# The tiles' transposes moved from TensorE to VectorE and a way through DRAM, in an attention and feed-forward kernel

## The chip, the cores and the metric

The kernel runs on one core of a Trainium2 chip. The metric is device time of one execution in microseconds (us). TensorE does the matrix products, VectorE and ScalarE work on tiles in on-chip memory (SBUF, 128 partitions) and on the matmuls' accumulators (PSUM, banks of 128 x 512 float32), GpSimd does elementwise work, and SyncE (SP) issues the transfers to and from DRAM, which 16 DMA engines carry out. Each engine works through its own instructions in order and waits on semaphores for the others.

## The reference

Everything is float32, with a batch of B = 2, T = 1024 tokens and C = 1024 channels:

```python
x = x + attn_a(layernorm(x))    # 32 heads of 32, causal, rope; plus a gated softmax over a prefix of 10 tokens
x = x + ffn(layernorm(x))
x = x + attn_b(layernorm(x))    # 8 heads of 16, not causal, softmax divided by sqrt(128)
x = x + ffn(layernorm(x))       # the same weights again

def attn_a(x):
    q, k, v = split(x @ w_attn.T, 3)                # 1024 columns each, in 32 heads
    y = softmax(causal(rope(q) @ rope(k).T / sqrt(32))) @ v
    y = y + gating * softmax(rope(q) @ ak.T / sqrt(1024)) @ av   # ak, av from the prefix
    return y @ w_proj.T

def ffn(x):
    base = x @ W_base.T + b_base
    w = sparsemax(x @ W_router.T + b_router)        # 8 experts
    h = einsum('bsd,edr->bser', x, lora_A)          # rank 16
    return base + einsum('bser,bse,ero->bso', h, w, lora_B)

def attn_b(x):
    q, k = (x @ Wqk_w.T + Wqk_b)                    # 128 columns each: 8 heads of 16
    v = x @ Wv_w.T + Wv_b                           # 128 columns
    return (softmax(q @ k.T) / sqrt(128) @ v) @ Wo_w.T + Wo_b
```

Every one of the four steps starts with a layer normalization over the channels, whose result has tokens on the partitions. The matrix products that follow contract over channels, so they need it the other way round, with channels on the partitions. How that turn is made is what the change is about.

## The kernel before

**Stages.** A tile is 128 tokens by 1024 channels, so each batch has NT = 8 tiles, and a tile has NC = 8 channel parts of 128. Stage A (attn_a, both batches, 8 groups of heads each) runs to about 1250 us, then its output projection to about 1460, the first feed-forward of batch 0 to about 1590, stage B's projection of batch 0 (`project_b`) to about 1645; from about 1690 attention B runs, with batch 1's first feed-forward and projection and much of the second feed-forward among it, and the end of the second feed-forward fills the time from about 2240.

**The order on TensorE** is written out ahead by a planner. Work around attention (projections, feed-forward) comes as generators which yield the estimated time of each matmul (a column costs COL = 1.7 ns); between attention's own steps `fill.run` takes so much of it. A few jobs are "chores", which are put off until they are due or until `flush` asks for them; a layer normalization's last part is such a chore, and `settle` flushes it. `pin` ties a VectorE instruction behind the latest softmax maximum.

**Two forms of a matmul.** `mm` (L195) issues one matmul of 128 columns of weights (L198) or, where the last thing before was a step of attention, four of 32 columns side by side (L200). `flip` (L202), a transpose by a matmul with the identity, sets it back to the first form. A float32 matmul shows as two records in the profile, so the second form shows as eight.

**Turning a tile.** `transposed` (L281) makes eight transposes by TensorE, in two banks of four (L204), and `evac` (L229) copies each bank into the turned tile, in turn by VectorE (L232) and ScalarE (L234). The turned tile has for every channel part 128 tokens side by side. All 64 tiles of the program are turned so: 16 in stage A, 32 in the two feed-forwards, 16 in stage B. In stage A, batch 1 is normalized early (`normalize_ahead`, L736), stored to DRAM (`xnd`, L741), loaded again (L751) and turned by `second` (L746) between matmuls, paced by `turn_over`.

**Feed-forward** (`ffn`, L1243). It works on pairs of tiles. `fetch` loads, `normalize` normalizes, `turn` (L1264) turns. `hidden` (L1312) makes hp, the experts' hidden values: for each tile eight matmuls with the turned tile's part as weights and 136 columns moving. The base product is made in seven products instead of eight (`seven_added`, L1069, in the order 1, 6, 2, 7, 5, 4, 3): `left_factors` (L1114) forms sums and differences of turned parts on VectorE, and the turned tiles are the weights of products with 512 columns moving. The next pair's tiles are turned inside products 5, 4 and 3.

**Stage B's projection** (`project_b`, L1470). For each tile eight matmuls make bv, with the turned tile's part as weights (L1504), and sixteen make bq, with it as the moving operand (L1525), 128 columns each.

**Transfers.** All are issued from SP, in program order. SP's rows in a profile are issues; a load that waits for something holds those behind it.

Of the kernel before, what the change touches and what calls it, by code (L numbers as in the profile page):

```python
# [20 lines left out]
P = 128  # L21
# [126 lines left out]
def tile_model(ctx: ExitStack, tc: tile.TileContext, d, out: bass.AP):  # L148
# [149 lines left out]


    class Unit:  # L300

# [261 lines left out]

    xnd = [dram.tile([P, C], F32, name=f"xnd{t}") for t in range(NT)]

    def stage_a(wk, big):
# [169 lines left out]
        def normalize_ahead():  # L736

            for t in range(NT + 1):
                if t:
                    settle(f"a1_{t - 1}")  # L740
                    sp.dma_start(xnd[t - 1], xn)  # L741
                if t < NT:
                    xn = layernorm(big, "t4k", x_load(1, t, big, "t4k"), f"a1_{t}", behind=True)
                yield ("norm", t)

        def second():  # L746


            def load(t):
                xn = big.tile([P, C], F32, tag="t4k", name=f"xn1_{t}")  # L750
                sp.dma_start(xn, xnd[t])  # L751
                return xn

            xns = {t: load(t) for t in range(2)}
            for t in range(NT):
                n, i = divmod(t, 4)
                if i == 0:
                    yield None
                    xnT[1, n] = big.tile([P, NC, HF], F32, tag="h16", name=f"xnT1_{n}")
                if t + 2 < NT:  # L760
                    xns[t + 2] = load(t + 2)
                yield from transposed(xns.pop(t), xnT[1, n][:, :, i * P : (i + 1) * P], f"a1_{t}")

        given = [False]
        owed = [0]

        def turn_over():

            owed[0] += 1
            if given[0]:  # L770
                given[0] = False
                return
            while owed[0]:
                owed[0] -= 1
                yield next(turnover)

        def adapter_scores(u):
            given[0] = True
            b, g, n = u.at
# [28 lines left out]
        def late(r, begun):  # L808
            spent = 0.0
            given[0] = False  # L810
            for u, at in begun.items():
                if r - at == 1:
                    spent += adapter_scores(u)
                elif r - at == 4:
                    spent += adapter_rows(u)
            return spent
# [62 lines left out]
        def project_first(b, between):  # L879
            wqk = wqk_at[b, 0]  # L880
            if b == 0:
                yield adapter_parts("k0", lambda c: wqk[:, c, 1, :], P)
            else:
                assert next(turnover) is None
                yield from begin_values(b, 0)
            for n in range(2):
# [6 lines left out]
                for s, key in ((1, "k"), (0, "q")):  # L893
                    qp = next_bank([P, HF], f"{key}p{b}_{n}")
                    for c in range(NC):
                        mm(qp, lhsT=wqk[:, c, s, :], rhs=xh[:, c, :], start=(c == 0), stop=(c == NC - 1))
                        yield HF * COL
                        if b and n == 0 and c % 2:
                            yield from turn_over()
                    rotate(b, 0, key, n, qp)  # L900
                    if b == 0 and n == 0 and key == "k":
                        yield adapter_keys(0)
                if b and n == 0:
                    while owed[0]:
                        owed[0] -= 1
                        yield next(turnover)
                yield ("qk", b, 0, n)
# [4 lines left out]
        def project_blocks(b, g):  # L912
            nm = f"{b}_{g}"
            k, q = st["k", b, g], st["q", b, g]
            if (b, g) == (0, NG - 1):
                assert next(turnover) is None
            halves = {i: (t, n) for i, t, n in ((11, k, 0), (12, k, 1), (21, q, 0), (22, q, 1))}
# [10 lines left out]
            for r in seven(b, nm, st.pop(("f", b, g)), mul, [P, HF], places, lambda x: rotate(b, g, "k", 0, x), settled):  # L928
# [3 lines left out]
                elif r is True:  # L932
                    yield ("qk", b, g, 0)
                else:
                    yield r
                    i += 1
                    if i == 14 and b == 0:
                        yield adapter_keys(g)
                    if (b, g) == (0, NG - 1) and i > 12 and i % 2 == 0:
                        yield from turn_over()  # L940
            while owed[0]:
                owed[0] -= 1
                yield next(turnover)
            yield ("qk", b, g, 1)
# [97 lines left out]
        ahead = normalize_ahead()  # L1042
        turnover = second()
        for b in range(B):
# [198 lines left out]
    def ffn(b, k, src, dst, w, wk, tiles, places, free=lambda: True, there=lambda t: True):  # L1243
# [6 lines left out]
        seq = [t for p in range(0, len(tiles), 2) for t in (tiles[p + 1], tiles[p])]  # L1250
        xs, xns, xts, hws, stores = {}, {}, {}, {}, deque()
        room = kept[2 if k else b]
# [6 lines left out]
        def normalize(i):  # L1259
            t = seq[i]  # L1260
            xns[t] = layernorm(wk, "xn", xs[t], f"f{b}_{k}_{t}", behind=True,
                               then=lambda: pool_add(xs[t], xs[t], w["b_base"]))

        def turn(i, parts=(0, 1), by=None):  # L1264
            t = seq[i]
            settle(f"f{b}_{k}_{t}")
            return transposed(xns[t], place_xt(i) if 0 in parts else xts[t], f"f{b}_{k}_{t}", parts, by)

        def place_xt(i):
            t = seq[i]  # L1270
            xts[t] = room["xt"] if room and i % 3 == 2 else wk.tile([P, NC, P], F32, tag="xt", name=f"xt_f{b}_{k}_{t}", bufs=2)
            return xts[t]

# [68 lines left out]
        def plain(p):  # L1342
            order = [(n, c) for n in range(2) for c in range(NC)]
            order = order[:4] + order[NC:] + order[4:NC]
            for i in range(2):
                t = seq[2 * p + i]
                ops = {}
                for n, c in order:
# [9 lines left out]
                    if (i, n, c) == (0, 1, 1):  # L1358
                        normalize(2)
                    if (i, n, c) == (1, 0, 1):  # L1360
                        while stores:
                            sp.dma_start(*stores.popleft())
                        fetch(3)
                    if (i, n, c) == (1, 1, 5):
                        normalize(3)
                    if i and c == 5:
                        yield from turn(2, (1 - n,))
                    if (i, n, c) == (0, 1, 5):
# [6 lines left out]
                    yield HF * COL  # L1375
            settle(f"f{b}_{k}_{seq[3]}")
            yield from transposed(xns[seq[3]], place_xt(3), f"f{b}_{k}_{seq[3]}", by=(next_bank, next_bank))

        def take_room():
            if not room or (b, k) == (1, 0):  # L1380
                ring, work, more = places()
                room.update(ring=ring, work=work, x=more[:, :2].rearrange("p a c -> p (a c)"),
                            xt=more[:, 2:].rearrange("p a (b c) -> p (a b) c", c=P))
                fill.flush("wb")
# [5 lines left out]
        yield None  # L1390
        normalize(0)
        yield None
        normalize(1)
        yield READY
        if not late_room:
            take_room()
        for i in range(2):
            yield from turn(i, by=(bank, next_bank))
        n_pairs = len(tiles) // 2
        for p in range(n_pairs):  # L1400
# [29 lines left out]
            hwT = []  # L1430
            turns = {(5, 0): (2, 0), (5, 3): (2, 1), (4, 2): (3, 0), (3, 1): (3, 1)}

            def ready(i):
                if i == 6:
                    fill.flush(nm)
                elif i == 5:
                    fill.flush("wb1")
                if not last and i in (6, 7):
                    normalize(2 * p + 2 + (i == 7))

            def also(i, k, dst):
                if not last and (i, k) in turns:
                    j, part = turns[i, k]
                    yield from turn(2 * p + j, (part,))
                if (i, k) == (2, 1):
# [24 lines left out]
    def project_b(b, w, fk, wk, st):  # L1470
        xs, ready = {}, {}

# [4 lines left out]
        def normalize(t):  # L1477
            xn = layernorm(fk, "xn", xs.pop(t), f"b{b}_{t}", behind=True)
            ready[t] = xn, fk.tile([P, NC, P], F32, tag="xt", name=f"xt_b{b}_{t}", bufs=2)

        fetch(0)
        fetch(1)
        yield None
        normalize(0)
        yield READY
        qk = st["qk", b] = wk.tile([P, 2, T], F32, tag=f"qkb{b}", name=f"qk{b}", bufs=1)
        kq = st["kq", b] = wk.tile([P, 2, T], F32, tag=f"kqb{b}", name=f"kq{b}", bufs=1)

        vm = st["vm", b] = wk.tile([P, NT, HB, 2 * EB], F32, tag=f"vm{b}", name=f"vm{b}", bufs=1)
        pool.memset(vm, 0.0)  # L1490
        normalize(1)
        fetch(2)
        fetch(3)
        settle(f"b{b}_0")
        yield from transposed(*ready[0], f"b{b}_0", by=(bank, next_bank))
        for t in range(NT):
            xnT = ready.pop(t)[1]
            if t >= NT - 2:

                yield AHEAD  # L1500
            cols = slice(t * P, (t + 1) * P)
            vp = next_bank([P, P], f"bv{b}_{t}")
# [10 lines left out]
            if t == NT - 2:  # L1513
                yield AHEAD
            if t + 1 < NT:
                settle(f"b{b}_{t + 1}")
                yield from transposed(*ready[t + 1], f"b{b}_{t + 1}", by=(bank, next_bank))
            if t + 2 < NT:
                normalize(t + 2)
            if t + 4 < NT:  # L1520
                fetch(t + 4)
            qp = next_bank([P, 2, P], f"bq{b}_{t}")
# [248 lines left out]
```

## Time and profile before

| | us |
|---|---|
| three runs | 2406.23, 2408.8, 2414.7 |
| median of these | 2408.8 |
| span of the profiled execution | 2407.9 |
| TensorE busy in it | 2351.2 (98%) |
| VectorE, ScalarE, GpSimd busy | 1437.3, 1100.4, 598.6 |
| moved by the DMA engines | 274.70 MB, 114 GB/s on the mean |

A row of a group names the line, the engine, the operation, output <- inputs with their shapes and the count of records; then the busy time of all, the mean of one in ns, and the idle time of the engine just before them with what ended it. Records of matmuls overlap, so the mean of one is longer than the time it takes of the order; a stretch of the timeline shows that.

By stage, the stretches that hold the tiles in question: in the first feed-forward of batch 0 (1460 to 1590 us) TensorE is busy for all of the 130 us, VectorE for 71.91, with the DMA engines at a share of 0.50; in 1855 to 1945 us, attention B with batch 1's projection, 85.00 of 90 and 71.38; in 2270 to 2408, the last feed-forward, 133.44 of 138 and 66.83. Much of SP's time is spent waiting for results to store.

### The profile page before, as it was taken

How to read it: one execution, taken by the hardware profiler on the slowest of the kernel's cores; microseconds unless marked ns; L12 is line 12 of the kernel's file. 1: busy time of each engine (PE TensorE's matmuls, PEld its weight loads, DVE VectorE, ACT ScalarE, POOL GpSimd, SP SyncE). 2: the span in 40 equal slices, each digit the busy share in tenths (PEclk: the TensorE clock that was granted, in tenths of full speed). 3: DMA queues.
4: the chain of work that ended last, by engine and by line, in shares of the span. 5: the costliest groups of instructions: out<-in, count | busy, mean ns of one | idle time of the engine just before them, and what ended most of it. 6: DMA issues, size and time to landing. Idle time of an engine off the chain costs nothing.

```text
span 2407.9 us, 60616 instructions
## 1 busy us (share of the span) xinstructions
PE 2351.2 (98%) x25151; PEld 1077.8 (45%) x25151; DVE 1437.3 (60%) x4317; ACT 1100.4 (46%) x2106; POOL 598.6 (25%) x933
## 2 busy tenths in 40 slices
PE   8999999999999999999999999999999999999999
PEld 4435443455354444445433445575333653233454
DVE  6587666666656666666651246566666765664453
ACT  3346665666565666666652001012455546564100
POOL 1432232222323232223211114202111111122332
PEclk9999999999999999999999999999999999999999
DMA  4443433333243333332312575441332302323543
GB/s 151 141 132 111 136 91 132 98 94 107 90 123 103 92 96 106 88 98 77 133 58 71 174 258 174 159 148 60 121 94 91 112 20 80 105 85 101 175 158 122
DMA packets 174772, 274.70 MB, mean 114 GB/s; under 512 B 16416, under 2 KB 76960, under 8 KB 174496
## 3 DMA queue, kind: packets, MB, share of 16 engines
q1 hardware_dynamic: 174496, 270.83, 35.2%
q8 instruction: 197, 3.23, 0.6%
q14 instruction: 79, 0.65, 0.1%
HBM read 215.19 MB, written 55.57 MB: 112 GB/s over the span
## 4 chain that ended last, share of the span: by engine, by line
PE 89%; DVE 6%; ACT 2%; DMA 1%; issue 1%; POOL 0%; SPq 0%; DVEq 0%; POOLq 0%; ACTq 0%
PE st L411 10%; PE sc L339 8%; PE y_A L433 5%; PE y L200 5%; PE y_f L198 4%; PE z_f L198 4%; PE z L200 4%; PE st L409 3%; PE x_f L198 3%; PE x L200 3%; PE y_v L200 3%; PE y_f L200 3%; PE y_B L433 2%; PE x_f L200 2%; PE y_p L198 2%; DVE pr_A L352 2%
## 5 line engine op out<-in xcount | busy, mean ns | idle before, releaser
L523 ACT ACTIVATE pt<-st 128x1024 f32<-128x1024 f32 (+1 forms) x418 | 425.5, 1018 | 605.8 <-PE st L411 463.6
L360 ACT ACTIVATE pr_A<-pr_A,nmax_A 128x896 f32<-128x896 f32 (+7 forms) x512 | 389.9, 765 | 55.1 <-DVE nmax_A L352 54.5
L352 DVE CUSTOM_DVE_ANT_0 pr_A<-sc,mask 128x512 f32<-128x512 f32 (+3 forms) x512 | 251.2, 537 | 190.2 <-PE st L411 90.7
L339 PE MATMUL sc<-kT,qT 32*128 32x512 f32 (+3 forms) x1536 | 326.1, 521 | 4.8 <-POOL qT L851 3.0
L411 PE MATMUL st<-qT,kT 32*128 32x512 f32 (+3 forms) x1536 | 306.4, 486 | 0.0
L352 DVE CUSTOM_DVE_ANT_0 pr_A<-sc,mask,part_A 128x512 f32<-128x512 f32 (+1 forms) x256 | 156.2, 647 | 145.7 <-PE sc L339 95.0
L418 POOL TENSOR_SCALAR_AFFINE_SELECT pt<-pt 128x256 f32<-128x256 f32 x256 | 105.9, 431 | 469.1 <-ACT pt L523 469.1
L239 POOL TENSOR_TENSOR xf<-xf,b_base 128x256 f32<-128x256 f32 x100 | 74.5, 775 | 417.8 <-DVE xn_f L267 261.9
L360 ACT ACTIVATE pr_B<-pr_B,nmax_B 128x1024 f32<-128x1024 f32 x128 | 145.5, 1141 | 36.4 <-DVE nmax_B L352 36.3
L433 PE MATMUL y_A<-pt,v 128*32 128x512 f32 (+3 forms) x1536 | 157.9, 498 | 0.0
L339 PE MATMUL sc<-kq,qk 32*128 32x512 f32 x512 | 146.5, 649 | 4.6 <-DVE nmax_B L352 3.8
L411 PE MATMUL st<-rows_B,kq 32*128 32x512 f32 x512 | 145.8, 646 | 2.4 <-ACT pt L523 1.7
L411 PEld LDWEIGHTS st<-qT,kT 32*128 32x128 f32 x1536 | 133.6, 185 | 16.3 <-issue 11.3
L409 PE MATMUL st<-rows_A,ones 3*128 3x512 bf16 (+3 forms) x768 | 127.8, 329 | 5.6 <-DVE nmax_A L352 5.0
L352 DVE CUSTOM_DVE_ANT_0 pr_B<-sc,zeros,part_B 128x512 f32<-128x512 f32 x128 | 91.0, 747 | 59.3 <-PE sc L339 59.3
L409 PEld LDWEIGHTS <-ones 3*128 3x128 bf16 x768 | 36.9, 91 | 194.7 <-issue 187.3
L339 PEld LDWEIGHTS sc<-kT,qT 32*128 32x128 f32 x1536 | 113.0, 184 | 18.3 <-POOL qT L851 5.0
L352 DVE CUSTOM_DVE_ANT_0 pr_B<-sc,zeros 128x512 f32<-128x512 f32 x128 | 83.2, 687 | 60.4 <-PE sc L339 60.2
L850 POOL TENSOR_TENSOR qr<-qr,sin 128x256 f32<-128x256 f32 x64 | 61.3, 957 | 220.9 <-DVE qr L846 213.9
L360 ACT ACTIVATION_READ_ACCUMULATOR pr_A<-pr_A,nmax_A 128x1 f32 x512 | 97.2, 190 | 0.0
L200 PE MATMUL y<-tt,wqk 128*32 128x512 f32 x768 | 92.6, 594 | 0.0
L433 PEld LDWEIGHTS y_A<-pt,v 128*32 128x32 f32 x1536 | 33.7, 108 | 118.2 <-issue 109.9
(424 smaller groups left out, 4232.8 us busy)
## 6 DMA issues: line engine op xcount, KB each, us to landing
tt<-td SPq DMA_DIRECT2D x252, 256.0 KB, 2.9
qkb_f<-tf SPq DMA_DIRECT2D x96, 256.0 KB, 3.0
qkb_s<-tf SPq DMA_DIRECT2D x84, 256.0 KB, 2.9
wqk<-in_w_attnT SPq DMA_DIRECT2D x32, 512.0 KB, 5.2
xf<-x SPq DMA_DIRECT2D x25, 512.0 KB, 3.7
xa<-in_x SPq DMA_DIRECT2D x16, 512.0 KB, 6.0
wv<-in_w_attnT SPq DMA_DIRECT2D x8, 1024.0 KB, 5.3
yd<-ys SPq DMA_DIRECT2D x32, 256.0 KB, 2.7
```

Source lines behind the costliest of these rows:

```text
L198: return pe.matmul(out, lhsT=lhsT, rhs=rhs, start=start, stop=stop, skip_group_check=True)
L200: pe.matmul(out[i : i + 32], lhsT=lhsT[:, i : i + 32], rhs=rhs, start=start, stop=stop, skip_group_check=True)
L239: pool.tensor_add(dst[:, i : i + 2 * P], a[:, i : i + 2 * P], b[:, i : i + 2 * P])
L339: yield w * COL, lambda: pe.matmul(dst[:, o : o + w], lhsT=self.qt[rows, qc : qc + P], rhs=self.kt[rows, c0 : c0 + w], start=True, stop=True)
L352: minimum[0] = dve.tensor_tensor_reduce(pr[:, c0 : c0 + w], sc[:, i, o : o + w], m, -self.scale, BIG if c0 == 0 else self.part[:, col], AL ...
L360: tc.keep_in_program_order(act.activation(pr[:, :nk], pr[:, :nk], AF.Exp, bias=self.nmax[:, col], scale=-1.0, accum_out=self.sums[:, col]))
L409: yield w * COL / 4, lambda: pe.matmul(dst[:, o : o + w], lhsT=of["ones"][three, :], rhs=self.rows[three, off : off + w], start=True, stop ...
L411: yield w * COL, lambda: pe.matmul(dst[:, o : o + w], lhsT=self.kt[rows, kb * P : (kb + 1) * P], rhs=rhs, start=self.extra, stop=True)
L418: pool.affine_select(out=dg, in_=dg, compare_op=ALU.is_ge, fill=0.0, base=0, pattern=[[0, 2], [1, P]], channel_multiplier=-1)
L433: pe.matmul(self.y[32 * h : 32 * h + 32, off : off + w], lhsT=self.value(h, kb), rhs=pt[h // 2][:, h % 2, o : o + w], start=self.opens, st ...
L523: act.activation(pt[:, :, low_:wide_], st[:, :, low_:wide_], AF.Exp, scale=ts[0][0].scale)
L850: pool.tensor_mul(qr[:, hs], qr[:, hs], sin[:, cols][:, hs])
```

## The change

56 of the 64 tiles are no longer turned by TensorE: the 8 of batch 1 in stage A, the 32 of the feed-forwards, the 16 of stage B. VectorE transposes the tile in blocks of 32 x 32 (`turned_out`), the result goes to a tile-sized place in DRAM, and it is read back so that the blocks land where a whole transpose needs them.

```diff
+    def turned_out(pl, tag, xn, dst, name, bufs=None, apart=True):
+        d = pl.tile([P, 4, P // 4 * NC], F32, tag=tag, name=f"d_{name}", **({"bufs": bufs} if bufs else {}))
+        blocks = d.rearrange("p b (i c) -> p c b i", c=NC) if apart else d.rearrange("p b (c i) -> p c b i", c=NC)
+        pin(dve.transpose(blocks, xn.rearrange("p (c b i) -> p c b i", b=4, i=32)))
+        sp.dma_start(dst, d.rearrange("p b e -> p (b e)"))
+
+    def turned_in(dst, src):
+        rows = src.rearrange("(a j) (b c i) -> a b j c i", a=4, b=4, i=32)
+        for b in range(4):
+            for a in range(4):
+                sp.dma_start(dst[32 * b : 32 * b + 32, :, 32 * a : 32 * a + 32], rows[a, b])
+
+    def turned_apart(pl, src, name):
+        xt = pl.tile([P, 4, P // 4 * NC], F32, tag="xt", name=f"xt_{name}", bufs=3) if not isinstance(pl, bass.AP) else pl
+        rows = src.rearrange("(a j) (b e) -> b j a e", a=4, b=4)
+        for b in range(4):
+            sp.dma_start(xt[32 * b : 32 * b + 32], rows[b])
+        return xt.rearrange("p a (i c) -> p c (a i)", c=NC)
```

In stage A (`apart=False`, `turned_in`) a tile is read back by 16 transfers of 32 KB, in runs of 32 elements, and the turned tile is laid out as before. `second(n)` issues those of four tiles in one go, 64 transfers; the transposes that `turn_over` spread between matmuls are gone:

```diff
+        def second(n):
+            xnT[1, n] = big.tile([P, NC, HF], F32, tag="h16", name=f"xnT1_{n}")
+            for i in range(4):
+                turned_in(xnT[1, n][:, :, i * P : (i + 1) * P], xnd[4 * n + i])
...
-                assert next(turnover) is None
+                second(1)
...
-                    if (b, g) == (0, NG - 1) and i > 12 and i % 2 == 0:
-                        yield from turn_over()
+                    if (b, g, i) == (0, NG - 1, 13):
+                        second(0)
```

In the feed-forward and in stage B (`turned_apart`) a tile is read back by four transfers of 128 KB in runs of 1 KB. For that the eight channel parts lie interleaved: element i of part c stands at 8 i + c, so every reader of a part, the matmuls and the VectorE operations of `left_factors`, reads it with a step of 32 bytes.

```diff
         def normalize(i):
             t = seq[i]
+            nm = f"f{b}_{k}_{t}"
+            xd = turning()
+            def rest():
+                pool_add(xs[t], xs[t], w["b_base"])
+                turned_out(wk, "xd", xns.pop(t), xd, nm, 2)
+            def place():
+                xts[t] = turned_apart(room["xt"] if room and i % 4 == 3 else wk, xd, nm)
+            xns[t] = layernorm(wk, "xn", xs[t], nm, behind=True, then=rest)
+            places_of[i] = place
...
-            turns = {(5, 0): (2, 0), (5, 3): (2, 1), (4, 2): (3, 0), (3, 1): (3, 1)}
...
-                if not last and i in (6, 7):
-                    normalize(2 * p + 2 + (i == 7))
+                if not last and i in (6, 2):
+                    normalize(2 * p + 2 + (i == 2))
+                if not last and i in (5, 3):
+                    turn(2 * p + 2 + (i == 3))
...
     def project_b(b, w, fk, wk, st):
...
+            if t + 2 < NT:
+                turn(t + 2)
...
-            if t + 2 < NT:
-                normalize(t + 2)
-            if t + 4 < NT:
-                fetch(t + 4)
+            if t + 3 < NT:
+                normalize(t + 3)
+            if t + 5 < NT:
+                fetch(t + 5)
```

So a tile is normalized before the second or third of the seven products and read back at the start of the fifth or the seventh; in `project_b` it is normalized three tiles ahead, read back two ahead, and loaded five ahead. Turned tiles have three buffers instead of two, and two buffers for the blocks are added; a scratch area that no transfer of this program uses is made smaller (`dynamic_dma_scratch_size=1024`). The eight tiles of batch 0 in stage A are turned by TensorE as before.

## The prediction

> **What bounds the kernel now.** I read the page's busy shares first, then the chain of waits, then the groups by form, then the stretches by stage and the timeline.
>
> ```profile
> span 2407.9 us, 60616 instructions
> PE 2351.2 (98%) x25151; PEld 1077.8 (45%) x25151; DVE 1437.3 (60%) x4317; ACT 1100.4 (46%) x2106; POOL 598.6 (25%) x933
> ...
> PE 89%; DVE 6%; ACT 2%; DMA 1%; issue 1%; POOL 0%; SPq 0%; DVEq 0%; POOLq 0%; ACTq 0%
> ```
>
> TensorE is busy 98% of the span and holds 89% of the chain that ended last, so a microsecond taken from its order is a microsecond of the end, and a microsecond added to it too. The work that the change removes (groups: count, then busy us and mean ns, then idle time before them and what ended it):
>
> ```profile
> L204 PE MATMUL xt_f<-ident,xn_f 128*128 128x128 f32 x256 | 38.1, 279 | 2.3 <-ACT xt_f L234 1.9 <-DVE xo L1555 0.4
> L204 PE MATMUL xt_b<-ident,xn_b 128*128 128x128 f32 x128 | 17.1, 276 | 2.7 <-DVE xn_b L267 1.8 <-DVE xo L1555 0.9
> L204 PE MATMUL xt_a<-ident,xn 128*128 128x128 f32 x64 | 10.8, 294 | 3.6 <-issue 1.5 <-DVE awTA L232 1.3 <-ACT xnT L234 0.7
> ...
> L232 DVE COPY xt_f<-xt_f 128x512 f32<-128x512 f32 x25 | 17.2, 689 | 18.1 <-PE xt_f L204 17.6
> ```
>
> These are the 448 transposes of the 56 tiles, 66.0 us of TensorE, with 8.6 us of idle time before them, and one of their evictions. How little room there is in the densest stage shows in TensorE's timeline (start, length):
>
> ```profile
> 1479.83 0.60 PE L204 MATMUL xt_f<-ident,xn_f 128*128 128x128 f32 x4
> 1480.27 2.74 PE L198 MATMUL z_f<-wb,kqb_f 128*128 128x512 f32 x6
> ```
>
> Four transposes hold TensorE's order for 0.44 us, from 1479.83 to the next start at 1480.27.
>
> **The change, part by part.**
>
> *Removed.* By the rows 66.0 us; by the order's pitch 112 groups of four times 0.44 us, or 49 us; among attention's matmuls the starts of such a group and the next instruction stand 0.49 us apart, which gives 55. With the waits in front it is 49 to 75. I take -60. The 56 evictions by VectorE (56 x 0.69 = 38.6 us) and the 56 by ScalarE go too; neither bounds.
>
> *Added on VectorE.* 56 block transposes of 128x1024. No such instruction is in the trace. Nearest are the shuffle of 128x512 at 732 ns and the pass of 128x1024 at 814 (L846 and L267). Below: 0.81 us, the pass. Above: two reads of the shuffle's kind, 1.46, plus 1024 x 0.65 ns for a stepped write (worked out next), 2.1 us. I take 1.7, so 95 us against 38.6 removed. The added products' subtractions (L1114) read the stepped tile: some 60 operations by 0.3 us, 18. VectorE goes from 1437 to about 1512 us, 63%: hidden by attention's and the dense matmuls' TensorE time. The cover is thin in one place only, stage B's dense projection:
>
> ```profile
> 1596.00:1642.00 46.00, 44.16 (x387) 43.01 (x386) 37.67 (x135) 6.75 (x22) 5.55 (x8) 1.00 0.37 126
> ```
>
> (length; busy time of TensorE, weight loads, VectorE, ScalarE, GpSimd; clock, DMA share, GB/s.) There a tile takes TensorE about 6.4 us (387 records at 56 a tile are 6.9 tiles in 44.16), of which 0.9 go, and VectorE near 6, to which about 0.7 net is added: eight tiles by 0 to 1.2 us. I take +5.
>
> *Added on the DMA queues.* Each of 48 tiles (feed-forward and stage B) is written in 512 KB and read back in four pieces of 128 KB. It adds 48 MB to 271, and SP issues five DMAs more per tile; the reads wait for the write, 3.0 us by the same write in stage A (xnd<-xn_a). SP's rows:
>
> ```profile
> 1218.34 4.21 SPq L1135 DMA_DIRECT2D yt<-yd  x8
> ...
> tt<-td SPq DMA_DIRECT2D x252, 256.0 KB, 2.9
> ```
>
> Eight in a row take 0.53 us each. In the feed-forward the second tile of a pair is the tight one: its reads are issued at the start of the last of seven products (four matmuls of 2 x 0.43 us, 3.4 us) and wanted after that product and the first tile's eight hp matmuls (8 x 2 x 0.116 = 1.9): 5.3 us, against 3 x 0.53 for the issues before the last and 2.1 to 2.9 for its landing, 3.7 to 4.5. I take 0, bounds 0 to 1 us a tile, 48.
>
> Stage A is different: `second(n)` puts 64 reads of 32 KB in one go on SP. At 0.45 to 0.53 us each they hold the queue for 29 to 34 us. The first burst starts near 544 us; behind it stands a load of tt that product y4 needs at about 560, and which lands at 544 + 29 + 2.9 = 576: a wait of 16. Behind the second burst (near 598) the tile is needed 28 us on, 0 to 9 late; I take 4. Together +20, bounds 5 to 45. [...] The trace's yt reads of 64 KB land in 2.1 us, not above the 2.9 of 256 KB, so I see a cost of issue and not of landing.
>
> *The 32-byte step on TensorE.* This decides. In the 48 tiles one channel part's 128 tokens now lie 32 bytes apart. The step is in the moving operand of 256 matmuls (bq), in the weights of 128 (bv) and 256 (hp), and in the weights of the base products, whose 512-column stream (0.43 us a record, two records) covers a load many times over: 0 for those. No operand of TensorE has a step in the trace. Rows:
>
> ```profile
> L198 PE MATMUL bq<-xt_b,wqk 128*128 128x128 f32 x384 | 47.0, 280 | 3.6 <-DVE mv_b L250 1.8 <-DVE r_f L266 0.9 <-DVE vm L1509 0.7
> L200 PE MATMUL bq<-xt_b,wqk 128*32 128x128 f32 x512 | 16.8, 285 | 0.0
> L200 PE MATMUL y<-tt,wqk 128*32 128x512 f32 x768 | 92.6, 594 | 0.0
> ...
> L597 DVE TENSOR_REDUCE tosum<-ident 128x10 f32<-128x40 f32 x1 | 0.2, 213 | 0.0
> L1293 DVE TENSOR_REDUCE cum_f<-prod_f 128x8 f32<-128x64 f32 x32 | 6.8, 211 | 0.0
> L1297 DVE TENSOR_REDUCE kz_f<-sup_f 128x1 f32<-128x8 f32 x32 | 5.0, 156 | 0.3
> ```
>
> VectorE has one: L597 reads 40 elements 128 bytes apart in 213 ns. Its contiguous relatives take 156 for 8 and 211 for 64, so 187 for 40: 26 ns over 40 elements, 0.65 ns each. A record of bq is 47.0/384 = 122 ns for 128 columns, so near 0.9 ns a column; a column that costs 0.6 more makes two records 0.15 us longer. Moving operand: 256 x 0.15 = 39 us. Weights: 384 x 0.15 = 58 if the load paces the matmul, 0 if the stream does; both are near 116 ns a record here, nothing tells, and I take half, 29. Sum +68. Ends: 0, and twice the time of all 640 in all their forms, 63.8 for bq, 31.9 for bv and 66.7 for hp: +162. For 0 speaks the y row: four streams of 32 columns run side by side (768 records in 92.6 us, 482 ns a group of four, against 472 ns for one whole record), so the operand's port has four times the reading in it that one stream needs. Against it: those streams are contiguous, and near half of bq's matmuls stay split after the change and would want four stepped streams at once. I go by VectorE's row.
>
> [...]
>
> *Sum.* 2407.9 - 60 + 5 + 20 + 68 = 2441. The profiled span is 0.9 us under the median of 2408.8, so no correction: 2440.
>
> **The rivals.**
>
> *The step is free on TensorE.* 2407.9 - 60 + 5 + 20 = 2373, faster; 2352 with the whole busy sum of 66 gained, 10 lost in stage A and none on VectorE; 2400 with stalls of 52. For it: the y row. It decides as soon as a stepped element costs TensorE less than about 0.17 ns: 28 us, what is left of -35 to the bound of 7 us, over 640 x 256 readings.
>
> *SP's queue.* The step is free, but the bursts cost 20 + 9 and a busier SP delays other loads by 1 us for each of 48 tiles: 2407.9 - 60 + 5 + 29 + 48 = 2430, slower. For it: loads of tt and of the feed-forward's factors are just in time on the same queue. Against: SP holds only 0% of the chain, DMA 1%.
>
> *VectorE becomes the bound.* Where softmax steps run, a block transpose of 2.1 us in front of a maximum that TensorE waits for costs up to 1 us on some 40 tiles: with a free step 2373 + 40 = 2413, no change. Against: VectorE's waits in the chain are 6% now.
>
> That the change does not do what it says I exclude: in the changed kernel's order on TensorE the 448 transposes are gone.
>
> **How the numbers follow.** What a measurement tells from no change is 0.3%, 7 us. The step costing: 0.46 (slower 0.44, same 0.02). The step free: 0.40 (faster 0.38, same 0.02). SP's queue 0.09 (slower 0.08, faster 0.01), VectorE 0.05 (slower 0.03, same 0.01, faster 0.01). That makes faster 0.40, same 0.05, slower 0.55. The likeliest case gives 2440, its own range 2405 to 2500: the step between +32 and +127; above that the weights would have to pay in full, which I leave out. The range must take in the free case: 2352 to 2500.
>
> **What would show it.** Right: bq's mean per record above 280 ns and its busy sum up by some 40 us from 63.8, hp's and bv's by half as much in proportion. Wrong: those three groups unchanged per matmul; then the span should lie near 2373, with TensorE's busy sum down by about 60. Stage A: a wait of TensorE of some 16 us near 560, ended by a load of tt or by SP's queue. VectorE: the block transpose's mean (0.81 to 2.1 us) and the idle time of TensorE in stage B's dense projection. SP: loads that end waits of TensorE in the feed-forward. The prediction is wrong if TensorE reads stepped operands at full pace, or if late tiles cost more than both bounds.

## The result, and the profile after

The changed kernel takes 2619.05 us (2616.18 to 2621.72, four runs), the kernel before beside it 2409.57: a ratio of 1.087, 95% interval 1.0847 to 1.0895. The profiled execution spans 2619.9 us, 212.0 more than that of before. The first lines of its page, and its chain of waits:

```profile
span 2619.9 us, 62029 instructions
...
PE 2472.1 (94%) x25597; PEld 1172.8 (45%) x25597; DVE 1520.8 (58%) x4317; ACT 1071.0 (41%) x2050; POOL 598.5 (23%) x933
...
PE 79%; DVE 11%; DMA 4%; SPq 2%; issue 1%; ACT 1%; POOL 0%; DVEq 0%; ACTq 0%; POOLq 0%
```

TensorE is busy for 120.9 us more although 66 us of transposes are gone, and idle for 91.1 us more (147.8 against 56.7). The two make the 212.0. In the chain, DMA and SP's queue have gone from 1% to 6% and VectorE from 6% to 11%. The busy time first: TensorE's group of hp in the form of 128 columns before, and then the groups by form after.

```profile
L198 PE MATMUL hp_f<-la,xt_f 128*128 128x136 f32 x248 | 30.7, 279 | 0.0
```

```profile
L198 PE MATMUL bq<-xt_b,wqk 128*128 128x128 f32 x262 | 62.4, 411 | 0.0
L200 PE MATMUL bq<-xt_b,wqk 128*32 128x128 f32 x1000 | 61.8, 411 | 0.0
L198 PE MATMUL hp_f<-la,xt_f 128*128 128x136 f32 x224 | 54.2, 401 | 11.2 <-DMA xt_f<-xtd 11.2
L198 PE MATMUL bv<-wv,xt_b 128*128 128x128 f32 x134 | 32.8, 400 | 1.7 <-DVE xn_b L267 1.7
L200 PE MATMUL hp_f<-la,xt_f 128*32 128x136 f32 x704 | 23.7, 281 | 0.0
L200 PE MATMUL bv<-wv,xt_b 128*32 128x128 f32 x488 | 16.3, 275 | 0.0
```

Divide busy time by records. A record of bq costs 238 ns instead of 122, and 62 instead of 33 in the form of four: the stepped moving operand is read at half the pace in both forms. hp and bv, stepped in the weights, go from 124 and 123 ns to 242 and 245 with 128 columns, but stay at 34 and 33 in the form of four, as before (35 and 32). With the few hp groups on other tiles, bq gained 60.4 us, hp 33.8 and bv 17.2, together 111. Less the 66 us of transposes that makes 45 of the 120.9. The other 76 us are spread over matmuls that take longer than before, at a granted clock of 0.968 on the mean instead of 0.995; the largest share is the products y_f, whose groups sum to 208.8 us instead of 184.5. The runs do not part the clock from what else lengthens them. TensorE's waits:

```profile
PE y_f L198 <- DMA qkb_f<-tf: 22.9, 8, 5.2
PE y L200 <- DMA tt<-td: 19.9, 1, 19.9
PE y_f L200 <- DMA qkb_f<-tf: 11.8, 5, 5.2
PE hp_f L198 <- DMA xt_f<-xtd: 11.2, 2, 9.7
PE y_f L198 <- DMA qkb_s<-tf: 10.2, 6, 3.3
```

(us in all, times, longest.) Each is a load that came late, and four of the five are not loads of turned tiles: 44.9 us for factors of the feed-forward's products, 19.9 for one load of tt in stage A. The reason for the factors shows in the first feed-forward. SP's timeline (start, length):

```profile
1518.54 0.32 SPq L306 DMA_DIRECT2D xtd<-d_f  x1
1518.97 1.20 SPq L1279 DMA_DIRECT2D qkb_f<-tf  x2
```

VectorE's:

```profile
1516.48 2.03 DVE L305 STREAM_TRANSPOSE d_f<-xn_f 128x1024 f32<-128x1024 f32 x1
```

And TensorE's:

```profile
1522.36 3.77 PE L198 MATMUL y_f<-qkb_f,xt_f 128*128 128x512 f32 x4 [5.17 <-DMA qkb_f<-tf]
```

The store of the blocks (L306) stands in SP's queue ahead of the loads of product 7's factors. It goes out at 1518.54, when VectorE's transpose ends; the loads behind it start at 1518.97 and TensorE, ready since about 1517.2, waits 5.17 us. Over the whole run SP stood 199.5 us at such stores of the feed-forward, much more than the 44.9 us that TensorE waited for factors, so not every one of them held back a load that was wanted:

```profile
SPq L306 <- DVE d_f L305: 199.5, 21, 30.5
```

### The profile page after: what moved, and what is told of

The parts are those of the page before. It is cut to its first block, busy times and chain, and to the rows that moved or that the text cites. A ratio compares the mean times of both kernels' runs of the same rounds, so it can differ in the third digit from the quotient of the medians.

```text
span 2619.9 us, 62029 instructions
## 1 busy us (share of the span) xinstructions
PE 2472.1 (94%) x25597; PEld 1172.8 (45%) x25597; DVE 1520.8 (58%) x4317; ACT 1071.0 (41%) x2050; POOL 598.5 (23%) x933
## 4 chain that ended last, share of the span: by engine, by line
PE 79%; DVE 11%; DMA 4%; SPq 2%; issue 1%; ACT 1%; POOL 0%; DVEq 0%; ACTq 0%; POOLq 0%
PE st L436 8%; PE sc L364 7%; PE y_A L458 5%; PE y L200 5%; PE y_f L198 4%; PE z L200 3%; PE st L434 3%; PE z_f L198 3%; PE x L200 3%; PE hp_f L198 3%; PE y_v L200 2%; SPq L314 2%; PE y_B L458 2%; PE bq L198 2%; PE bq L200 2%; PE z_f L200 2%
## 5 line engine op out<-in xcount | busy, mean ns | idle before, releaser
L364 PE MATMUL sc<-kq,qk 32*128 32x512 f32 x512 | 149.6, 661 | 11.1 <-DVE part_B L377 8.1
L200 PE MATMUL y<-tt,wqk 128*32 128x512 f32 x808 | 98.7, 599 | 19.9 <-DMA tt<-td 19.9
```

Source lines behind the costliest of these rows:

```text
L200: pe.matmul(out[i : i + 32], lhsT=lhsT[:, i : i + 32], rhs=rhs, start=start, stop=stop, skip_group_check=True)
L364: yield w * COL, lambda: pe.matmul(dst[:, o : o + w], lhsT=self.qt[rows, qc : qc + P], rhs=self.kt[rows, c0 : c0 + w], start=True, stop=True)
```

## The experiments

"Before" beside the runs was 2411.85 for e1 to e4, 2412.1 for e5 to e8, 2411.7 for e9 to e12 and 2412.86 for e13 and e14.

**e1: the step alone.** TensorE still turns; only the layout changes.

```diff
-wk.tile([P, NC, P], F32, tag="xt", name=f"xt_f{b}_{k}_{t}", bufs=2)
+wk.tile([P, P, NC], F32, tag="xt", name=f"xt_f{b}_{k}_{t}", bufs=2).rearrange("p i c -> p c i")
...
-fk.tile([P, NC, P], F32, tag="xt", name=f"xt_b{b}_{t}", bufs=2)
+fk.tile([P, P, NC], F32, tag="xt", name=f"xt_b{b}_{t}", bufs=2).rearrange("p i c -> p c i")
```

> The kernel before, with one thing changed: the turned tiles of the feed-forward and of stage B are laid out with their eight channel parts interleaved (the two evictions write with a 32-byte step); TensorE still turns them, nothing goes through DRAM. Theory 1 (the step doubles what TensorE reads in bq, and in the weights of hp and bv where they are loaded 128 columns at a time): the three groups go from 162 us of busy time to about 270, and the time from 2409 to 2510-2550 us. Theory 2 (the step costs only beside the new transfers, or the records of after are long because the tiles are late): the three groups stay below 180 us and the time below 2440 us.

Measured: 2540.67 us, ratio 1.0526 (1.0505 to 1.0546), +129 us. Its groups on TensorE:

```profile
L198 PE MATMUL bq<-xt_b,wqk 128*128 128x128 f32 x384 | 92.1, 412 | 3.3 <-DVE mv_b L250 2.2 <-DVE vm L1509 1.2
L198 PE MATMUL hp_f<-la,xt_f 128*128 128x136 f32 x248 | 60.9, 401 | 0.0
...
L200 PE MATMUL hp_f<-la,xt_f 128*32 128x136 f32 x608 | 21.5, 281 | 0.0
```

240 and 246 ns a record, and 35 in the form of four: the doubling needs neither the new transfers nor late tiles. TensorE stays busy for 98% of that run, at a clock of 0.996. Theory 1 held. In this run the three groups gained 118 us (bq 60, hp 38, bv 20), since more of hp and bv is in the 128-column form than in the changed kernel. The base products gained 5 (x_f on a turned tile went from 460 to 475 ns a record in the first feed-forward). That is the 123 us by which this run's profiled execution is longer.

**e2: runs of 32 in place of the step.** Each channel part's tokens lie as four runs of 32, so nothing reads with a step of 32 bytes; where they are weights, this kernel loads them run by run, 32 columns at a time.

```diff
-return xt.rearrange("p a (i c) -> p c (a i)", c=NC)
+return xt.rearrange("p a (c i) -> p c a i", c=NC)
...
-        if not split[0]:
+        runs = len(lhsT.shape) == 3
+        if not (split[0] or runs):
...
+            part = lhsT[:, i // 32, :] if runs else lhsT[:, i : i + 32]
```

> The changed kernel without the step: a channel part's 128 tokens lie as four runs of 32 floats side by side (1 KB apart), read back in the same four transfers with 1 KB runs. Weights with such runs are always loaded in the form of four matmuls of 32 columns. Theory 1: bq, hp and bv go back to about 162 us, the waits for transfers stay, and the time falls from 2619 by 100-130 us to 2490-2520 us. Theory 2 (SP's queue and late tiles are most of the loss): the time stays above 2570 us.

Measured: 2528.16 us, 1.0474 (1.0454 to 1.0494): 91 less than the changed kernel, somewhat short of the 100 to 130 expected, and nearer to theory 1. bq is back at 64 us. The waits for factors remain (37 us), and the stretches show what a pause costs besides itself: the first feed-forward takes 162 us (132 before), of which 18.8 are such waits, at a granted clock of 0.92.

**e3 and e4: stage A.** e3 is the changed kernel with stage A's functions of before; e4 the kernel before with stage A's functions of the change.

```diff
 # e4, stage A only
-                assert next(turnover) is None
+                second(1)
...
+                    if (b, g, i) == (0, NG - 1, 13):
+                        second(0)
```

> The changed kernel with stage A as before (its eight tiles turned by TensorE again). The wait of 19.9 us for a load of tt goes, 10.8 us of transposes come back: a gain of 5 to 15 us on 2619, 2604 to 2614 us. A rival, that the burst delays much more than that one load, gives a gain over 25 us.

> The kernel before with stage A's part of the change alone (eight tiles through DRAM in 128 transfers of 32 KB, no 32-byte step). By the waits of after: +19.9 for tt, +2.7 for the second burst, -10.8 of transposes: 2409 + 12, 2415 to 2428 us. If VectorE's transposes or the longer queue cost more: above 2430; if the wait has cover: at or under 2405.

Measured: e3 2592.26 us, 27 less than the change; e4 2438.85 us, 1.011 (1.0095 to 1.0125), 27 more than before. By their own kernels before, the two say 29 and 27. Both lie where the rival of each text stands, over 25 and above 2430: the burst, or what comes with it, costs more than that one wait. e8 tells which. SP's queue in e4, and then four stretches of 10 us there (length; busy time of TensorE, weight loads, VectorE, ScalarE, GpSimd; granted clock; DMA share, GB/s):

```profile
557.39 32.77 SPq L314 DMA_DIRECT2D xnT<-xnd  x64
590.26 2.29 SPq L654 DMA_DIRECT2D tt<-td  x5
```

```profile
560.00:570.00 10.00, 10.00 (x106) 3.06 (x98) 4.59 (x17) 6.00 (x13) 1.14 (x2) 1.00 0.38 60
570.00:580.00 10.00, 3.50 (x32) 0.68 (x24) 3.53 (x8) 3.97 (x7) 3.35 (x4) 0.82 0.43 67
580.00:590.00 10.00, 0.00 (x0) 0.00 (x0) 0.00 (x0) 0.00 (x0) 0.00 (x0) 0.50 0.42 66
590.00:600.00 10.00, 6.90 (x44) 1.78 (x44) 1.31 (x4) 1.02 (x1) 0.00 (x0) 0.66 0.68 210
```

The burst holds SP for 32.77 us, 0.51 a read; the load of tt goes out at 590.26; from 580 to 590 no engine does anything, while the DMA engines are at a share of 0.42: the cost is in the issue and not in moving the data. And the clock granted to TensorE falls to 0.50 in the pause and is still at 0.66 on the mean of the next stretch.

**e8: the burst spread.** Stage A's part as in e4, with 16 reads at a time.

```diff
-                    if (b, g, i) == (0, NG - 1, 13):
-                        second(0)
+                    if (b, g) == (0, NG - 1) and i in (13, 17, 21, 25):
+                        second(0, (i - 13) // 4)
```

> The kernel before with stage A's part of the change alone, its 128 reads not in two bursts of 64 but in eight of 16, four matmuls apart. Theory (the burst of 33 us on SP holds one load of tt back for 20 us and TensorE's clock falls in that pause): the wait of 19.6 us goes, and the time falls from 2439 to 2400-2415 us. Rival (VectorE's eight transposes or the reads themselves cost it): 2430 us or above.

Measured: 2418.05 us, 1.0019 (1.0005 to 1.0032). The wait of 19.6 us is gone and with it 21 of e4's 27 us, so the burst is the cause of those 21. It ends above the expected band: a loss of 6 against before stays, though 10.8 us of transposes are gone. TensorE's waits for the partial maxima of the softmax of stage A (part_A, nmax_A) are 16.9 us here, 6.7 before; VectorE's eight transposes stand earlier (at 139 to 464 us in the changed kernel), and why these waits grew was not traced.

**e5: stepped weights in four.** The changed kernel, with the step.

```diff
-        if not split[0]:
+        if not (split[0] or lhsT.ap[-1][0] != 1):
```

> The changed kernel, with the 32-byte step kept, but every matmul whose weights are read with the step is issued as four of 32 columns. Theory (a stepped 128-column load takes 334 ns instead of 190 and is not covered, a stepped 32-column load takes 140 instead of 110 and is): hp and bv, 103 us in the 128-column form, take 57 in the other; bq, whose step is in the moving operand, stays at 124 us. The time falls from 2619 by 35 to 60 us to 2560-2585 us. Rival (the step costs per element read, in whatever form): hp and bv stay near 150 us in all and the time at 2610 us or above.

Measured: 2591.7 us, 1.0734 (1.0705 to 1.0762).

```profile
L200 PE MATMUL hp_f<-la,xt_f 128*32 128x136 f32 x1600 | 53.4, 286 | 9.6 <-DMA xt_f<-xtd 9.6
```

33 ns a record, no dearer than weights without a step. The loads of weights show why; hp's before and in the changed kernel, in both forms:

```profile
L198 PEld LDWEIGHTS hp_f<-la,xt_f 128*128 128x128 f32 x248 | 29.8, 190 | 1.4 <-issue 1.4
L200 PEld LDWEIGHTS hp_f<-la,xt_f 128*32 128x32 f32 x608 | 17.7, 110 | 9.1 <-issue 9.0
```

```profile
L198 PEld LDWEIGHTS hp_f<-la,xt_f 128*128 128x128 f32 x224 | 54.8, 334 | 15.3 <-issue 14.3
L200 PEld LDWEIGHTS hp_f<-la,xt_f 128*32 128x32 f32 x704 | 21.1, 139 | 9.8 <-issue 9.7
```

In the 128-column form the loads are busy for 54.8 us with the step, as long as the matmuls themselves (54.2), so they set the pace. hp and bv take 101 us in all instead of 150. The time fell by 27 us, below the expected 35 to 60: the waits for factors are still there, and the form of four has a price of its own (e10).

**e6 and e7: the stores later on SP.** The kernel of e2, its stores issued from another place in SP's order; e7 also has stage A as before.

```diff
-                if not last and i in (5, 3):
-                    turn(2 * p + 2 + (i == 3))
+                if not last and i == 5:
+                    put(2 * p + 2)
+                if not last and i == 4:
+                    turn(2 * p + 2)
+                    put(2 * p + 3)
+                if not last and i == 3:
+                    turn(2 * p + 3)
```

`put` issues the store that stood behind the transpose. The first tile's reads move one product back with it. Stage B puts at the start of the step and reads back after bv.

> The kernel of the runs of 32 (2528 us), with the stores of the blocks moved behind on SP: in the feed-forward the first tile's store goes behind the factor loads of product 7 and the second's behind those of product 4, in stage B's projection a store goes one step ahead of its reads. Theory (a store that waits for VectorE's transpose holds back the loads behind it on SP): the waits of TensorE for qkb loads, 37 us there, fall under 12 us, TensorE's clock in the dense stretches goes from 0.90-0.92 back to above 0.95, and the time falls by 40 to 80 us to 2450-2490 us. Rival (the queues or DRAM traffic themselves are too slow): the waits stay and the time stays above 2510 us.

> The same with stage A turned by TensorE as before. Theory: stage A's loss of 27 us goes too: 27 to 34 us less than the run with the stores moved alone, 2420-2460 us; at best, with no waits left, 2412 - 49 = 2363 us.

Measured: e6 2475.16 us, 1.025 (1.0214 to 1.0287), 53 less than e2; e7 2443.64, 1.0133 (1.0099 to 1.0167), 32 less again. Of e6's waits for factors this is left:

```profile
PE y_f L202 <- DMA qkb_f<-tf: 0.4, 1, 0.4
```

And the first feed-forward in e2, then in e6:

```profile
1498.00:1660.00 162.00, 143.22 (x1258) 52.07 (x1256) 78.45 (x235) 8.09 (x30) 33.97 (x48) 0.92 0.60 186
```

```profile
1490.00:1624.00 134.00, 133.89 (x1257) 50.48 (x1256) 79.84 (x235) 8.12 (x30) 34.36 (x48) 1.00 0.71 225
```

It is back at 134 us and a clock of 1.00, while the DMA engines move 225 GB/s there, more than in e2 (186). So neither the DMA engines nor DRAM were too slow; the order on SP was wrong.

**e9: no turn at all.** The most that the idea can give.

```diff
+            if not name.startswith("a0"):
+                evac(dst[:, 4 * j : 4 * j + 4, :], xn[:, 4 * j * P : (4 * j + 4) * P].rearrange("p (a b) -> p a b", b=P))
+                yield 0.0
+                continue
```

> The kernel before without the turn of the 56 tiles: their 448 transposes on TensorE are left out, the evictions copy the normalized tile as it lies, so the matmuls work on tiles that are not turned. Nothing else is changed: this is the most that taking the transposes from TensorE can give. Theory (TensorE bounds everywhere, as the prediction has it): 49 to 75 us less than 2410, 2335-2361 us. Rival (in attention B the matmuls around softmax wait for it, and work taken out of there is not a shorter end): 2365-2390 us.

Measured: 2355.42 us, 0.9767 (0.975 to 0.9783), 56 less than before. Theory held: attention B, 507 us before, takes 485 there.

**e10: the form of four in the kernel before.**

```diff
-        if not split[0]:
+        if not (split[0] or four):
```

> The kernel before, with all matmuls whose weights are a turned tile of the feed-forward or of stage B issued as four of 32 columns, as in the runs of 32. Theory (the form of four is a few per cent slower in the dense stretches, 3.91 us against 3.71 for 16 matmuls of hp, 3.54 against 3.43 for 4 of 512 columns): 8 to 20 us more than 2410. Rival: the form costs nothing, within 5 us.

Measured: 2441.15 us, 1.0124 (1.0109 to 1.0139), +29 us, above both theories. Weights without a step have a price too. For e2, e6 and e7 it is less than 29: e10 puts the form also into stage A's output projection, which is made by the same seven products and stays whole in those three. It takes 219 us in e10 instead of 213 (from its first x_p to the first hp_f), which leaves about 23.

**e12, e13, e14: VectorE's transposes alone.** The kernel before with 48 block transposes added, unused; with the step in their output (e12), without it (e13), with it and in four pieces (e14).

```diff
+        d = pl.tile([P, 4, P // 4 * NC], F32, tag="xd", name=f"d_{name}", bufs=2)
+        pin(dve.transpose(d.rearrange("p b (i c) -> p c b i", c=NC), xn.rearrange("p (c b i) -> p c b i", b=4, i=32)))
 # e14
+        for c in range(0, NC, 2):
+            fill.chore(("ln", name), lambda c=c: pin(dve.transpose(to[:, c : c + 2], at[:, c : c + 2])))
```

> The kernel before with VectorE's block transpose of each of the 48 tiles of feed-forward and stage B added, its result unused, some 48 x 2.05 = 98 us more of VectorE. Theory (hidden but for stage B's dense projection): 0 to 10 us more than 2410. Rival (it delays the maxima that TensorE waits for and the normalizations): over 20 us.

> The kernel before with the 48 unused block transposes on VectorE, written in runs of 32 in place of the 32-byte step, 1.24 us each where the stepped ones took 2.06 (which added 41 us). Theory (VectorE's time itself is paid where softmax's maxima stand behind it, so the cost goes with the length): 20 to 28 us more than 2411. Rival (a fixed delay for each instruction, whatever its length): 38 us or more. Second rival (only what is longer than the room between two maxima is paid): under 12 us.

> The kernel before with the 48 unused stepped block transposes, each in four pieces of 256 channels that are put between other work of VectorE. Theory (the time is paid whatever its cut): 35 to 48 us more than 2411. Rival (a maximum that waits behind one long instruction is the cost): under 20 us.

Measured: e12 2453.02 us, 1.0174 (1.0159 to 1.0189), +41; e13 2426.38, 1.0055 (1.0036 to 1.0074), +14; e14 2428.36, 1.0067 (1.0045 to 1.0089), +16. e12 met its rival (over 20) and e14 its own (under 20); e13 lies between its second rival (under 12) and its theory (20 to 28). Two stretches (project_b up to attention B, and attention B) before, then in e12, and one group of e14:

```profile
1592.00:1741.00 149.00, 146.35 (x1190) 84.57 (x1187) 106.79 (x352) 42.72 (x90) 26.10 (x36) 1.00 0.33 105
1741.00:2248.00 507.00, 493.06 (x4804) 191.82 (x4800) 314.25 (x929) 271.51 (x424) 95.23 (x131) 0.98 0.27 88
```

```profile
1600.00:1759.00 159.00, 148.14 (x1185) 85.51 (x1184) 127.46 (x363) 42.42 (x89) 26.05 (x36) 0.99 0.31 99
1759.00:2287.00 528.00, 505.48 (x4800) 194.06 (x4800) 346.77 (x949) 271.89 (x424) 94.25 (x131) 0.98 0.25 85
```

```profile
L304 DVE STREAM_TRANSPOSE d_f<-xn_f 128x256 f32<-128x256 f32 x128 | 72.6, 636 | 0.4
```

VectorE is busy for 66% of attention B in e12, and yet attention B takes 528 us instead of 507, and stage B's projection 159 instead of 149. In pieces the transposes take more of VectorE in all (106 us against 99) and cost less than half, so it is not their sum that is paid. That it is the length of one instruction is what e13 points to: at the same places, 1.24 us each instead of 2.06 cost a third. e14's pieces also stand at other places, between other work, and no run parts length from place. How the time is lost shows only in part: TensorE's waits for the maxima (part_B, nmax_B) in attention B rise from 4.6 to 10.4 us, of the 21 lost there.

**e11: the later pairs alone.** Only the later tiles of the feed-forwards go through DRAM; stage A, stage B and the first two tiles of each feed-forward are turned by TensorE.

> The change kept only for the later pairs of tiles of the feed-forwards: stage A, stage B and the first two tiles of every feed-forward are turned by TensorE as before, the stores go behind the factor loads, the 32-byte step stays but hp is issued as four of 32 columns where it reads it. Theory: of some 24 tiles 0.9 us each goes, 21 us, and the stepped weights and the form of four give 10 back: 2395-2405 us. Rival (the way through DRAM still comes late): above 2415 us.

```diff
-        turn(0)
-        turn(1)
...
+            yield from transposed(xns[t], xts[t], f"f{b}_{k}_{t}", by=(bank, next_bank))
```

Measured: 2423.15 us, 1.0047 (1.0031 to 1.0062), 11 more than before and in the rival's range, but not by the rival's cause: none of TensorE's waits of 1.9 us and more in this run ends with a load. The first feed-forward and the last stretch gain 3 us each, and attention B loses 13; TensorE's waits for its maxima (part_B, nmax_B) are 14.5 us there, 4.6 before, with VectorE's stepped transposes (2.06 to 2.07 us each in e12) in the program. No version that turns its tiles beat the kernel before.

## Why the prediction was right or wrong

Right was the sign, the step of 32 bytes as its largest term, and the bound: TensorE's order is worth what it was said to be, -56 (e9) against -60. The measured time lies 119 us above the end of the range. The step as it measured alone (+129) brings the prediction's own sum to 2502, the end of its range; two terms that it put at next to nothing do the rest. Its rivals were weighed one against the other, two of them with a free step, and the step, SP's queue and VectorE all came at once. Term by term:

| term | predicted | measured alone | by |
|---|---|---|---|
| transposes gone | -60 | -56 | e9 |
| 32-byte step | +68 | +129 | e1 |
| stage A's bursts | +20 | +38 (27, and the 10.8 of transposes that it saves) | e4 |
| transfers of the 48 tiles | 0 | +53 | e6 against e2 |
| VectorE | +5 | +41 | e12 |

The measured column makes +205, beside the +209 of the result. That the terms add up so closely is partly luck: e12 keeps the evictions that the change drops, e6 against e2 was measured without the step, and the same reckoning misses e7 by some 43 us (below).

*The 32-byte step.* The mechanism was right and the size was off. "A column that costs 0.6 more" was VectorE's row; TensorE pays a whole column more (122 to 238 ns a record), and the moving operand cost 60 us in e1 where 39 were taken. "I take half, 29" for the weights fell too: in the 128-column form they are paid in full, 58 us in e1. The range ended where the weights pay in full, "which I leave out". What was argued for a free step, that four streams have four times the reading in them, says nothing on a step: in the form of four every stream is halved alike. Weights taken 32 columns at a time do not pay: their load grows (110 to 139 ns) but stays covered, and a record of hp takes 33 ns in e5 and 34 in the changed kernel, 35 before.

*The DMA queues.* This step failed: "I take 0, bounds 0 to 1 us a tile". It reckoned how long a tile's own reads take to land. The loss lies with others: the store, which waits for VectorE, holds back the factor loads queued behind it. The question of what is queued behind a waiting instruction was put for stage A's burst and not for the stores. The rival of SP's queue named those loads and a price near the measured one, 48, but not the store, at a chance of 0.09.

*VectorE.* This step failed: "hidden by attention's and the dense matmuls' TensorE time". The duration lay in its bounds (2.06 us where 1.7 was taken and 2.1 was the upper end); the cover was read from a share of busy time, 63%. Of e12's 41 us, 10 lie in the stretch of stage B's projection, where 5 were taken, and 21 in attention B, where none were. The third rival had nearly the price, "up to 1 us on some 40 tiles", and a mechanism that e13 and e14 support, at a chance of 0.05.

*Stage A.* The wait was foreseen at 16 us near 560 and came at 19.6, from 573 to 593 in e4: right in its cause, and the term of 38 lies within its bounds of 5 to 45. The burst is 21 of it, by e8; what the other 17 are was not foreseen and is not traced further than the longer waits for maxima there.

*Open.* e7, with no step, no burst and the stores later, is still 32 us above before. Its form of four (23, e10), its transposes (14, e13) and 48 less on TensorE (48 of e9's 56 tiles) leave about 43 us. In stage B's stretch, 168 us against 149, TensorE waits 11.1 us for a first tile and 9.7 before bv, at a clock of 0.95; the rest was not traced to a cause.

## What to carry to other kernels

Ask of each added transfer not only when its data land, but what it waits for at the head of its queue and which loads stand behind it: moving the stores, and some of the reads with them, was worth 53 us. Look at the step of an operand before looking at runs of a transfer, since the matmuls that read a tile pay for its layout each time (129 us in e1). And where a chain of short steps runs through an engine that is 60% busy, try long added instructions in pieces: whole they cost 41 us here, in pieces placed between other work 16.

## What the runs showed of the hardware

- A moving operand of float32 with a 32-byte step is read at half the pace: 122 to 238 ns a record of 128 columns, and 33 to 62 in the form of four, where each of four streams side by side is halved.
- Weights with that step: a load of 128 columns goes from 190 to 334 ns and paces the matmul (124 to 242 ns a record); one of 32 columns goes from 110 to 139 ns and does not show.
- A block transpose of 128x1024 float32 on VectorE takes 1.24 us with runs of 32 in its output and 2.06 with the 32-byte step; a quarter of it with the step takes 0.63.
- A pause of 20 us takes TensorE's granted clock to 0.50; in the dense stretches of the changed kernel, with waits for late loads of up to 10 us in them, it is 0.91 to 0.92 on the mean.
- 64 reads of 32 KB in a row go out at 0.51 us each, and the DMA engines are at a share of 0.42 while everything waits for SP.
